# Layer 0 of a two-layer transformer kernel: attention and its following blocks traced in the order of a clock kept in the kernel

## The chip, the cores and the metric

The kernel runs on one core of a Trainium2 chip. A core has five engines that run side by side, each working through its own queue strictly in order: TensorE (PE, matrix products and transposes; weight loads are shown apart as PEld), VectorE (DVE), ScalarE (ACT), GpSimd (POOL) and SyncE (SP, which here only issues DMAs). ACT and POOL issue some DMAs too. Engines wait for each other through semaphores. The metric is the device time of one execution in microseconds (us).

## The reference, cut to what matters

The input x has 4 sequences of 512 positions and 512 features. Four blocks follow each other; every one is `x = x + layernorm(f(layernorm(x)))`, and layernorm has no gain or bias:

```python
x = x + _layernorm(_L0_attn_ref(_layernorm(x), Wq, Wkv, Wo))        # 32 heads of 16, one shared k and v, ALiBi, causal
x = x + _layernorm(_L0_ffn_ref(_layernorm(x), q_scales, q_vals, bias))  # one dequantised 512x512 product plus a bias
x = x + _layernorm(_L1_attn_ref(_layernorm(x), Wq, Wkr, Wdk, Wupk, Wupv, Wo))  # 32 heads of 128, 8 key heads, rope
x = x + _layernorm(_L1_ffn_ref(_layernorm(x), w_gate, w_up, w_down))    # gated, ternary octonion weights
```

Everything is float32. A product in the kernel takes both factors as a rounded high part and a low part and sums three matmuls (high by high, high by low, low by high).

## The kernel before, in words

The program is unrolled in Python and then ordered per engine by a scheduler in the compiler, which follows the order of tracing as a priority and simulates the engines. So the order in which Python emits instructions matters, but an engine's queue may differ from it.

There are three phases. Phase A (classes `A1` and `A2`) does all of layer 0, and also the weight products and the value projection of layer 1's attention. Phase B (`phase_b`) does layer 1's attention and phase C (`C`) its feed-forward block. In the profile phase B's first matmul stands at 727.8 us, and phase A's last matmuls lie just behind it.

**Attention in phase A.** A batch (sequence) has four groups of eight heads, m = 0 to 3. `front` normalises and transposes a batch's x and makes keys and values, `qproj` makes the queries of one group and stores them in DRAM, and `qload` loads them back, rearranged, into the buffer `QS[m]`. The scores are computed twice. `max_tile` (L422, L426) makes them with queries on the partitions, and DVE reduces each tile to a row maximum (L430). `max_end` transposes 32 columns of maxima (L439) and writes them by an ACT-issued DMA into a row of `QS`, so that a second product gives scores with the maximum already taken off. `exp_tile` makes that product with keys on the partitions (L467), ACT takes the exponential (L470), and POOL masks the diagonal tile (L472). `pv` multiplies by values (L483), and `o_piece` transposes the result back (L500) and divides by the sum. There are 128 steps u (a head for the maxima, a block of keys for half a group for the exponentials).

**Posts.** `A2.post(b, t)` takes 128 rows through everything that follows: product with Wo, `add_norm`, feed-forward product with bias (L818), `add_norm`, storing x2 and the transposed normalised x, and two value products for layer 1. `add_norm` is a chain: DVE statistics, aggregate and an add (`ln_gen`, L102 to L106), a power on POOL (L108), a tiny DVE operation (L111), ACT scales and shifts (L727), POOL adds the residual (L729), a second `ln_gen`, and ACT again (L733). `A2.weights` makes combined weights for layer 1 (`products`) and splits the weights of the posts (`setup`); posts wait for it.

**What sets the order.** All of this work is Python generators. `A1.run` walks u from 0 to 140 with the exponentials a fixed 12 steps behind the maxima (`LAG`), four sub-steps each; in each sub-step it emits one maximum tile, gives every waiting generator one turn (`slot`), emits one exponential tile, and gives another turn. A generator spaces itself by counting turns: `hop(n)` lets n turns pass. The exponential tiles have a raised priority (`prio`). Two post streams share the first three batches' twelve posts, and the four posts of the last batch run as four generators with banks and buffers of their own (`room`).

**Banks.** PSUM has eight banks: three for maxima (`ps`), two for exponentials (`pt`), one for probability-by-value sums (`po`), two (`mm`) for everything else. After step 130 three in five exponential tiles take a `ps` bank. `Tok` counts free banks and buffers.

Of the kernel before, what the change touches and what calls it, by code (L numbers as in the profile page):

```python
# [20 lines left out]
B, S, D = 4, 512, 512  # L21
NT = B * S // 128
# [64 lines left out]
class Hop:  # L87

    fine = True

    def __call__(self, n, coarse=0):
        for _ in range(n if self.fine else coarse):
            yield


hop = Hop()


def ln_gen(nc, c, pool, src):

    st = pool.tile([128, 6], F32, name="ln_st", tag="ln_st")
# [7 lines left out]
    yield from hop(3)  # L109
    nm = pool.tile([128, 1], F32, name="ln_nm", tag="ln_nm")  # L110
    nc.vector.scalar_tensor_tensor(nm, mv[:, 0:1], -1.0, rs, ALU.mult, ALU.mult)  # L111
    return rs, nm


class Tok:


    def __init__(self, n):
        self.n = n

    def take(self):
        while self.n == 0:
            yield
        self.n -= 1

    def give(self):
        self.n += 1


class Bank:  # L130
# [9 lines left out]
    def give(self):  # L140
        self.tok.give()


def transpose_gen(nc, c, bank, src, dst_h, dst_l):
    ps = yield from bank.take([128, KC, 128])
    for k in range(KC):
        nc.tensor.transpose(ps[:, k, :], src[:, bass.ts(k, 128)], c.ident)
    yield from hop(1)
    nc.scalar.copy(dst_h, ps)
    yield from hop(2)  # L150
    nc.vector.tensor_tensor(dst_l, ps, f(dst_h), ALU.subtract)
    bank.give()
    yield from hop(1, 1)


def mm3_gen(nc, ps, lh, ll, rh, rl, ks, hops=2, stop=True):
    n = len(ks)
    for j, k in enumerate(ks):
        nc.tensor.matmul(ps, lh(k), rh(k), start=(j == 0), stop=False)  # L159
        nc.tensor.matmul(ps, lh(k), rl(k), start=False, stop=False)  # L160
        nc.tensor.matmul(ps, ll(k), rh(k), start=False, stop=(stop and j == n - 1))  # L161
        yield from hop(hops)
# [24 lines left out]
class Gens:  # L187


    def __init__(self):  # L190
        self.q = []

    def add(self, *gs):
        self.q += gs

    def step(self, n=1):
        for _ in range(n):
            if not self.q:
                return
            g = self.q.pop(0)  # L200
            try:
                next(g)
                self.q.append(g)
            except StopIteration:
                pass

    def drain(self):
        while self.q:
            self.step()


# [4 lines left out]
class A1:  # L216


    def __init__(self, tc, nc, c, aps, o_d, xtp, wqp, P):
# [14 lines left out]
        self.mmp = c.mmp  # L234
# [4 lines left out]
        self.projected = self.exped = self.maxed = self.fronted = self.turn = self.ended = 0  # L239
# [60 lines left out]
    def front(self, b, x):  # L300
# [3 lines left out]
        if x is None:  # L304
# [3 lines left out]
            yield from hop(8)  # L308
        while self.projected < 4 * b:
            yield  # L310
# [3 lines left out]
        for t in range(4):  # L314
# [8 lines left out]
            yield from hop(2)  # L323
# [6 lines left out]
        else:  # L330
# [3 lines left out]
                           lambda k: xt_h[:, k], lambda k: xt_l[:, k], range(KC))  # L334
        vt = self.qp.tile([32, S], F32, name="vt", tag="ql")
        nc.scalar.copy(vt, ps[32:64])
        yield
        for two in range(2):
# [3 lines left out]
            yield from hop(3)  # L342
# [3 lines left out]
            yield  # L346
        if spare:
            psv = self.psT.tile([128, 4, 32], F32, name="ptv", tag="pt")
        else:
            tok.give()  # L350
            yield from tok.take()
            psv = mmp.tile([128, 4, 32], F32, name="mmv", tag="mm")
        for t in range(4):
            nc.tensor.transpose(psv[:, t], vt[:, bass.ts(t, 128)], c.ident[:32, :32])
        vx = self.vp.tile([128, 4, 32], F32, name="vx", tag="vx")
        nc.gpsimd.memset(vx, 1.0)
        yield
        nc.vector.tensor_copy(vx[:, :, 0:16], psv[:, :, 16:32])
        if not spare:
            tok.give()  # L360
        self.vx[b] = vx

    def qproj(self, b, m):
        nc = self.nc
        while self.fronted <= b:
            yield
# [6 lines left out]
        self.projected += 1  # L373
        qh = self.qp.tile([128, S], F32R, name="qh", tag="qh")
        nc.scalar.copy(qh, ps)
        yield from hop(2)
        ql = self.qp.tile([128, S], F32R, name="ql", tag="ql")
        nc.vector.tensor_tensor(ql, ps, f(qh), ALU.subtract)
        self.tok.give()
        dh = self.dp.tile([128, S], F32, name="qh_d", tag="qh_d")  # L380
        nc.sync.dma_start(dh, f(qh))
        dl = self.dp.tile([128, S], F32, name="ql_d", tag="ql_d")
        nc.sync.dma_start(dl, f(ql))
        self.q_d[b, m] = dh, dl

    def qload(self, b, m):
        nc = self.nc
        while (b, m) not in self.q_d:
            yield
        dh, dl = self.q_d.pop((b, m))  # L390
        while self.exped < 32 * (b - 1) + 8 * m + 8:
            yield
# [16 lines left out]
    def max_tile(self, b, m, j, q):  # L409

        nc = self.nc
        two, pr = j // 4, j % 4
        ks = self.KS[b]
        if j == 0 and q == 0:
            assert (b, m) in self.queries
            self.mn = self.sm.tile([128, 8, 4], F32, name="mn", tag="mn", bufs=2)
# [10 lines left out]
        for jj, qb, p in todo + [(j, qb, p)]:  # L427
            nk = 128 * (qb + 1)
            jk = self.jp.tile([128, 512], BF, name="jk", tag="jk")
            nc.vector.tensor_tensor_reduce(  # L430
                out=jk[:, :nk], in0=p, in1=self.c.mask[:, 384 - 128 * qb:512],
                scale=-1.0, scalar=3e38, op0=ALU.add, op1=ALU.min,
                accum_out=self.mn[:, jj, qb:qb + 1])

    def max_end(self, m, mn):
        nc = self.nc
        yield from self.tok.take()
        pm = self.mmp.tile([32, 128], F32, name="mm", tag="mm")
        nc.tensor.transpose(pm, mn.rearrange("p a b -> p (a b)"), self.c.ident)  # L439
        yield  # L440
        mt = self.sm.tile([32, 128], F32R, name="mt", tag="mt", bufs=2)
        nc.scalar.copy(mt, pm)
        self.tok.give()
        for two in range(2):
            r = 64 * two + 58
            nc.scalar.dma_start(f(self.QS[m][r:r + 1]), f(mt[16 * two:16 * two + 16]))
        self.maxed += 8

    def exp_tile(self, v, q):
# [945 lines left out]
```

## Time and profile before

| | us |
|---|---|
| median of 3 runs | 2410.93 (2410.16 to 2412.91) |
| profiled execution | 2413.31 |
| its span, first to last instruction | 2411.6 |
| PE busy in the span | 2301.8 (95%) |
| DVE busy | 1573.0 (65%) |
| POOL busy | 1190.3 (49%) |
| ACT busy | 1076.9 (45%) |
| first score matmul of layer 0 (L422) | at 40.2 |
| first post's first transpose (L147 on po_ot) | at 263.9 |
| last maximum tile (L426) | at 582.4 |
| last exponential tile (L467) | at 667.1 |
| first key projection of layer 1 (L182 on wk_h) | at 727.8 |

The profile is of one execution. A line of a group names the kernel's line, the engine, the operation, output and inputs with shapes, the count, then busy us, mean ns of one, and the idle time of that engine just before, with what ended it. PE's matmuls are pipelined and their ends are modelled, so PE's busy time is an upper bound of its work. The granted clock (PEclk) is the share of full speed that PE was given.

### The profile page before, as it was taken

What the parts mean: (1) busy time and instruction counts of PE and PEld (TensorE: products, weight loads), DVE (VectorE), ACT (ScalarE), POOL (GpSimd) and SP (SyncE); (2) the same over time, 40 slices, a digit from 0 to 9 for tenths busy, and PEclk for the clock granted to TensorE, in tenths of its full rate; (3) what the DMA queues carried; (4) which work ended last, traced back from release to release, by engine and by line L of the source; (5) the groups of instructions that cost most, each with busy time, mean ns of one, the idle gap of its engine ahead of it and who ended that gap; (6) DMA issues with size and microseconds to landing.
All of it is one profiled execution on the core that took longest, in us unless ns stands there. A gap on an engine that the chain in (4) does not pass through costs nothing.

```text
span 2411.6 us, 35873 instructions
## 1 busy us (share of the span) xinstructions
PE 2301.8 (95%) x11606; PEld 1794.2 (74%) x11606; DVE 1573.0 (65%) x4631; ACT 1076.9 (45%) x2404; POOL 1190.3 (49%) x1387
## 2 busy tenths in 40 slices
PE   6899889988889999999999999999999999999998
PEld 4566455555557788888888888888888888878886
DVE  7766656555356777777777767777777778764443
ACT  3555445545543344444444444444444445453332
POOL 3323333434343676566566566666656667522221
PEclk8899899999999999999999999999999999999999
DMA  8845434343367432233122222232222222041000
GB/s 183 238 145 181 98 92 111 89 106 110 94 188 207 135 103 75 88 101 102 66 88 105 70 88 97 79 106 70 88 97 79 91 85 79 14 127 57 31 27 18
DMA packets 158558, 241.54 MB, mean 100 GB/s; under 512 B 26738, under 2 KB 91506, under 8 KB 149540
## 3 DMA queue, kind: packets, MB, share of 16 engines
q1 hardware_dynamic: 141748, 202.42, 27.9%
q0 software_dynamic: 14768, 35.92, 5.3%
q8 instruction: 93, 1.52, 0.3%
q10 hardware_dynamic: 1856, 0.92, 0.2%
q14 instruction: 93, 0.76, 0.1%
HBM read 183.17 MB, written 63.92 MB: 102 GB/s over the span
## 4 chain that ended last, share of the span: by engine, by line
PE 84%; issue 4%; DMA 4%; DVE 3%; POOL 2%; ACT 2%; SPq 1%; ACTq 0%; POOLq 0%; DVEq 0%
PE mm L182 11%; PE mm L184 11%; PE mm L183 11%; PE pt L989 6%; PE mm L159 3%; PE pt L467 3%; PE po L483 3%; PE po L1002 3%; PE po L1003 3%; PE mm L161 3%; PE po L1004 3%; PE mm L160 3%; PE ps L969 3%; PE ps L970 3%; PE ps L971 3%
## 5 line engine op out<-in xcount | busy, mean ns | idle before, releaser
L980 POOL TENSOR_TENSOR s<-s,r 128x384 f32<-128x384 f32 (+3 forms) x512 | 359.6, 722 | 130.0 <-DVE r L979 119.7
L977 ACT ACTIVATE s<-s,mn 128x384 f32<-128x384 f32 (+3 forms) x512 | 286.0, 560 | 223.8 <-DVE mn L973 215.9
L863 POOL TENSOR_TENSOR rp_a<-rp_a,rp_b 128x512 f32<-128x512 f32 x155 | 200.3, 1292 | 262.3 <-DVE rp_b L862 247.5
L992 ACT CAST ph<-pt 128x512 fp32r<-128x512 f32 x320 | 181.7, 586 | 295.5 <-PE pt L989 287.8
L430 DVE CUSTOM_DVE_ANT_0 jk<-ps,mask 128x384 bf16<-128x384 f32 (+3 forms) x512 | 227.5, 483 | 81.2 <-PE ps L426 72.1
L993 DVE TENSOR_TENSOR pl<-pt,ph 128x512 fp32r<-128x512 f32 x320 | 216.5, 686 | 43.4 <-ACT ph L992 40.4
L973 DVE CUSTOM_DVE_ANT_0 s<-ps,mask 128x384 f32<-128x384 f32 (+2 forms) x384 | 203.1, 552 | 37.7 <-PE ps L971 19.5
L470 ACT ACTIVATE pe<-pt 128x512 f32<-128x512 f32 x307 | 174.4, 600 | 97.0 <-PE pt L467 92.7
L989 PE MATMUL pt<-ident,s 128*128 128x128 f32 x1280 | 214.1, 272 | 0.7 <-POOL s L980 0.5
L182 PE MATMUL mm<-xh,w_h 128*128 128x512 f32 x512 | 205.4, 401 | 2.1 <-DVE rp_b L862 1.9
L182 PE MATMUL mm<-w_h,oh 128*128 128x512 f32 x512 | 203.7, 398 | 0.7 <-ACT oh L1008 0.7
L184 PE MATMUL mm<-xh,w_l 128*128 128x512 f32 x512 | 203.6, 398 | 0.0
L183 PE MATMUL mm<-xl,w_h 128*128 128x512 f32 x512 | 202.1, 395 | 0.0
L183 PE MATMUL mm<-w_l,oh 128*128 128x512 f32 x512 | 201.7, 394 | 0.0
L184 PE MATMUL mm<-w_h,ol 128*128 128x512 f32 x512 | 200.3, 391 | 0.0
L989 PEld LDWEIGHTS pt<-ident,s 128*128 128x128 f32 x1280 | 164.7, 140 | 46.1 <-POOL s L980 1.1
L865 POOL TENSOR_TENSOR ql<-rp_a,qh 128x512 fp32r<-128x512 f32 x124 | 160.5, 1294 | 49.6 <-ACT qh L864 49.6
L472 POOL TENSOR_SCALAR_AFFINE_SELECT pe<-pe 128x512 f32<-128x512 f32 x128 | 82.5, 647 | 195.7 <-ACT pe L470 195.1
L859 DVE TENSOR_TENSOR rp_a<-mm,cosq 128x512 f32<-128x512 f32 x128 | 88.4, 691 | 119.6 <-PE mm L184 94.3
L426 PE MATMUL ps<-KS,QS 128*128 128x256 f32 (+2 forms) x384 | 132.7, 384 | 19.2 <-DVE mn L430 18.7
L108 POOL TENSOR_TENSOR ln_rs<-ln_ve,mhalf 128x1 f32<-128x1 f32 x112 | 63.8, 575 | 173.0 <-DVE ln_ve L106 145.5
L1008 ACT CAST oh<-po 128x512 fp32r<-128x512 f32 x128 | 74.5, 582 | 166.1 <-PE po L1004 165.9
(359 smaller groups left out, 5872.5 us busy)
## 6 DMA issues: line engine op xcount, KB each, us to landing
xh<-xt SPq DMA_DIRECT2D x32, 1024.0 KB
xl<-xt SPq DMA_DIRECT2D x32, 1024.0 KB
vh<-v SPq DMA_DIRECT2D x32, 256.0 KB
vl<-v SPq DMA_DIRECT2D x32, 256.0 KB
raw<-in_a_wo SPq DMA_DIRECT2D x32, 256.0 KB
w_h<-in_a_wo POOLq DMA_DIRECT2D x32, 256.0 KB, 3.2
m_d<-t_d SPq DMA_DIRECT2D x192, 42.5 KB
QS<-qh_d SPq DMA_DIRECT2D x62, 128.0 KB
```

Source lines behind the costliest of these rows:

```text
L182: nc.tensor.matmul(ps, lh(k), rh(k), start=(j == 0), stop=False)
L183: nc.tensor.matmul(ps, lh(k), rl(k), start=False, stop=False)
L184: nc.tensor.matmul(ps, ll(k), rh(k), start=False, stop=(j == n - 1))
L430: nc.vector.tensor_tensor_reduce(out=jk[:, :nk], in0=p, in1=self.c.mask[:, 384 - 128 * qb:512], scale=-1.0, scalar=3e38, op0=ALU.add, op1= ...
L470: nc.scalar.activation(e, ps, AF.Exp)
L863: eng.tensor_tensor(a, a, r, ALU.add)
L973: nc.vector.tensor_tensor_reduce(out=s[:, :nk], in0=ps[:, :nk], in1=mask, scale=-1.0, scalar=3e38, op0=ALU.add, op1=ALU.min, accum_out=mn)
L977: nc.scalar.activation(s[:, :nk], s[:, :nk], AF.Exp, bias=mn, scale=-1.0, accum_out=l)
L980: nc.gpsimd.tensor_tensor(s[:, :nk], s[:, :nk], r.to_broadcast([128, nk]), ALU.mult)
L989: nc.tensor.transpose(pt[:, j], PS[u, qb, j][:, bass.ts(kb, 128)], c.ident)
L992: nc.scalar.copy(ph, pt)
L993: nc.vector.tensor_tensor(pl, pt, f(ph), ALU.subtract)
```

## The change

The change replaces the hand-counted order of phase A by a list order made while tracing.

- `Clock` holds a time for each engine and, for each tile, when it was last written and last read. `lengths` gives a duration for each instruction from its engine and its free size, `book` advances the engine and the tiles. `TimedCore` wraps the engines so that every instruction in phase A's `run` is booked, and also chained by `issue_after` behind the previous one on its engine: the compiler's scheduler can no longer change the order within phase A. `TimedPool` gives a reused buffer the time at which its oldest use ends.
- `Streams.run` holds ranked generators. At each turn it takes the generator of best (lowest) rank whose inputs are ready by the clock at PE's time; if none is, it moves to the soonest. `wait(n, tiles)` yields the time the tiles are ready; without a clock (before `run`, and in phases B and C) it lets n turns pass as `hop` did.
- Ranks: query and value weight loads 0; reductions and exponentials on DVE and ACT 1; row maxima and probability-by-value 2; projections, weights, head outputs and posts 3; the maxima's matmuls 4, or 6 when they are `LEAD` = 14 steps ahead of the exponentials; the exponentials' matmuls 4. `LAG`, `slot`, `prio` and the borrowed `ps` banks go.
- Four post streams, one for each row block t, go through all four batches in the same code. They share three pairs of transposed tiles and, for the first three batches, the two `mm` banks; the last batch's streams have a bank each.
- `add_norm` no longer forms the shifted sum: one DVE operation makes `y * rs + x`, which differs from it by a constant per row, and the next normalisation removes that constant. The two shifts are added back once, when x2 is stored, by one extra ACT pass and one tiny DVE add per post.

```diff
+LEAD = 14
+class Clock:
+    def ready(self, *aps):
+        return max((self.done.get(a.tensor.name, 0.0) for a in aps), default=0.0)
+    def lengths(self, e, op, out, ins, kw):
+        n = out.free_size()
+        if op == "dma_start":
+            issue = {self.SP: 0.4, self.ACT: 0.55, self.POOL: 0.7}[e]
+            return issue, issue + 2.2 + 4e-5 * out.size() / 4
+        if e == self.PE:
+            n = 0.108 if op == "transpose" else 0.018 + 0.417e-3 * n
+            return n, n + 0.2
+        if e == self.ACT:
+            n = 0.2 + 0.78e-3 * n + 0.2 * (len(ins) > 2)
+            return n - 0.12, n + 0.03
+        if e == self.DVE:
+            n = 0.15 + 1.05e-3 * max(n, max((a.free_size() for a in ins), default=0))
+            return n - 0.08, n + 0.03
+        n = 0.56 if n == 1 else 0.05 + (1.15e-3 if op != "tensor_tensor" else 2.4e-3) * n
+        return n - 0.05, n + 0.08
...
+class Timed:
...
+            with ck.tc.issue_after(ck.last[e]) if e in ck.last else nullcontext():
+                r = fn(*a, **k)
+            ck.last[e] = r.ins
+            ck.book(e, op, outs, pos + ins, k)
...
+class Streams:
+    def run(self):
+        ck = self.ck
+        while self.q:
+            now, best, soonest = ck.now(), None, float("inf")
+            for s in sorted(self.q, key=lambda s: (s[0](), s[1])):
+                t = s[3]() if s[3] else 0.0
+                if t < soonest:
+                    best, soonest = s, t
+                if t <= now:
+                    break
+            ck.t = max(now, soonest)
+            try:
+                best[3] = next(best[2])
+            except StopIteration:
+                self.q.remove(best)
...
-    def run(self, extra):
-        LAG = 12
-        total = 32 * B
-        self.gens += [self.projections(), self.loads()]
-        for u in range(total + LAG + 1):
...
+    def run(self, ck, starts):
+        self.nc = TimedCore(ck, self.nc)
+        self.streams = Streams(ck)
+        self.rank = self.streams.add
+        self.begun = lambda u: [self.rank(*g) for g in starts.get(u, [])]
+        for m in range(4):
+            ck.done[self.QS[m].tensor.name] = 3.0 * m
+        self.rank(0, self.loads())
+        self.rank(2, self.outputs())
+        self.rank(3, self.projections())
+        self.rank(lambda: 4 if self.heads < self.exped + LEAD else 6, self.maxima())
+        self.rank(4, self.exponentials())
...
-    def add_norm(self, y, x, bank, o, new_xn):
+    def add_norm(self, y, x, bank, o):
         nc, c = self.nc, self.c
-        rs, nm = yield from ln_gen(nc, c, self.sm, y)
-        o = o()
-        nc.scalar.activation(o, y, AF.Identity, bias=nm, scale=rs)
-        bank.give()
-        nc.gpsimd.tensor_tensor(o, o, x, ALU.add)
-        rs, nm = yield from ln_gen(nc, c, self.sm, o)
-        xn = new_xn()
-        nc.scalar.activation(xn, o, AF.Identity, bias=nm, scale=rs)
+        rs, mv = yield from rstd_gen(nc, c, self.sm, y)
+        yield from wait(1, rs, x)
+        nc.vector.scalar_tensor_tensor(o, y, rs, x, ALU.mult, ALU.add)
+        bank.give(y)
+        shift = ln_shift(nc, self.sm, rs, mv)
+        rs, mv = yield from rstd_gen(nc, c, self.sm, o)
+        yield from wait(1, rs)
+        return shift, rs, ln_shift(nc, self.sm, rs, mv)
...
     def post(self, b, t):
...
-        x2, xn = yield from self.add_norm(y, x1, bank, r.x2, r.n2)
-        out = nc.sync if last else nc.gpsimd
-        out.dma_start(self.x2_d[bass.ts(T, 128), :], x2)
-        xh, xl = yield from r.pair("x2")
-        yield from transpose_gen(nc, c, bank, xn, xh, xl)
+        s2, rs, nm = yield from self.add_norm(y, y1, bank, x)
+        yield from wait(0, nm)
+        nc.scalar.activation(y1, x, AF.Identity, bias=nm, scale=rs)
+        shift = self.sm.tile([128, 1], F32, name="shift", tag="shift")
+        nc.vector.tensor_tensor(shift, s1, s2, ALU.add)
+        xh, xl = yield from self.pair()
+        yield from transpose_gen(nc, c, bank, y1, xh, xl)
+        nc.scalar.activation(x, x, AF.Identity, bias=shift)
...
     def posts(self):
-        todo = [(b, t) for b in range(B - 1) for t in range(4)]
-        def stream():
-            while todo:
-                yield from self.post(*todo.pop(0))
-        return [stream(), stream()] + [self.post(B - 1, t) for t in range(4)]
+        def stream(t):
+            for b in range(B):
+                yield from self.post(b, t)
+        return [(3, stream(t)) for t in range(4)]
...
-            start = {4: [a2.weights()], 5: [a2.load_wv()], 6: a2.posts()}
-            a1.run(lambda u: start.get(u, []))
+            a2 = A2(tc, TimedCore(ck, nc), c, aps, a1, o_d, x2_d, xt_d, v_d, wk_d, wv_d, P1)
+            a1.run(ck, {4: [(3, a2.weights())], 5: [(0, a2.load_wv())], 6: a2.posts()})
```

## The prediction

> **What bounds the kernel now.** First the page's row of slices: after slice 13 (about 780 us) TensorE (PE) is 90% busy or more in every slice, and those two thirds are not in the diff. Before, it falls to 8, and its granted clock with it.
>
> ```profile
> PE   6899889988889999999999999999999999999998
> PEclk8899899999999999999999999999999999999999
> ```
>
> So I cut layer 0 into windows (columns: stretch, length, busy us and instructions of PE, PEld, DVE, ACT, POOL, then PE clock, DMA share, GB/s).
>
> ```profile
> 100.00:720.00 620.00, 560.57 (x3028) 357.46 (x3028) 355.04 (x1355) 309.30 (x559) 220.79 (x305) 0.96 0.45 124
> 140.00:220.00 80.00, 79.86 (x450) 56.11 (x449) 45.93 (x173) 38.58 (x72) 15.13 (x20) 1.00 0.43 133
> 240.00:280.00 40.00, 32.06 (x162) 16.65 (x159) 25.04 (x109) 16.39 (x30) 12.26 (x16) 0.83 0.51 122
> 580.00:720.00 140.00, 117.36 (x577) 76.07 (x577) 55.76 (x154) 64.11 (x109) 58.56 (x79) 0.94 0.46 139
> ```
>
> PE leaves 59 us idle in 100-720, but busy overstates: an isolated matmul is drawn 0.40 long, while in an unbroken run the next starts after 0.23. I therefore count work by spacing at full clock, from PE's timeline of 100-720: 1360 matmuls 512 wide at 0.233 (starts 590.87 to 592.27, six of them) make 317; 77 of 384 at 0.178, 14; 205 of 256 at 0.12, 25; 339 transposes at 0.09, 30; the probability-by-value groups at 0.99, 0.78, 0.57 and 0.35 per eight, 86. That is **472 us of work in 620 us: 0.76**. The same count gives 0.94 for 140-220 (projections, weight products and attention all ready), 0.79 for 300-580, 0.54 for 240-280 (attention alone) and 0.69 for 580-720. DVE is at 57%, ACT 50%, POOL 36%: no engine but PE is near its limit, so the lost 148 us are order and latency.
>
> Who holds PE, from the waits of 100-670 (us in total, times, longest):
>
> ```profile
> PEld ps L426 <- DVE mn L430: 31.1, 53, 6.5
> PEld pt L467 <- ACT pe L470: 22.1, 46, 1.1
> PEld mm L147 <- ACT xn L733: 16.6, 8, 4.5
> ```
>
> These are the maxima's and exponentials' banks, and transposes behind a norm: each a matmul queued before its input while other work was ready. Two places in the timeline show what that costs. First, a load holds DVE at the head of its queue, and all engines stop for 6.5 us:
>
> ```profile
> 247.51 1.06 PE L483 MATMUL po<-pe,vx 128*32 128x512 f32 x8
> ...
> 252.93 0.69 DVE L718 SCALAR_TENSOR_TENSOR x<-x,xn 128x512 f32<-128x512 int32 x1 [7.06 <-DMA xn<-in_f_s]
> ...
> 254.15 1.41 PE L426 MATMUL ps<-KS,QS 128*128 128x384 f32 x2 [5.58 <-DVE mn L430]
> ```
>
> Second, two short gaps halve the clock (starts 0.43 apart):
>
> ```profile
> 643.96 0.66 PE L147 MATMUL mm<-ident,xn 128*128 128x128 f32 x4 [1.70 <-ACT xn L733]
> 645.56 0.80 PE L159 MATMUL mm<-wv_h,x2h 128*128 128x512 f32 x1 [0.95 <-ACT x2h L149]
> 646.16 0.63 PE L160 MATMUL mm<-wv_l,x2h 128*128 128x512 f32 x1
> 646.59 0.63 PE L161 MATMUL mm<-wv_h,x2l 128*128 128x512 f32 x1
> ```
>
> Over 100-720 the clock shortfall in 20 us windows sums to 28 us.
>
> **The change part by part.** The sum is made against the profiled execution: 2413.3 us, span 2411.6 and 1.7 around it; the median of the runs is 2410.9, 2.4 less.
>
> *Order (the main term).* No matmul is added or removed. The kernel's clock traces an instruction when its inputs are done by its own account, and chains each engine to that order. Its durations fit the rows: exponential 0.60 booked, 0.60 measured; 512-wide DVE subtract 0.69 and 0.69; POOL add 1.28 and 1.28; pow 0.56 and 0.57; matmul 0.23 and 0.23; SP issue 0.4 and 0.42. The last 50 us of work are the final batch's four posts, four alike chains in both orders; 680-720 ran at 0.70, I take 0.75 for a shorter chain: 50/0.75 = 67. The other 422 us lie between 0.79, where posts and attention mix today (no gain), and 0.94, where enough is ready. I take the middle, 0.865, because the clock removes waits for DVE and ACT but not the chains: 488. Together 555 against 620: **65 us less**.
>
> *Normalisation.* By group rows of 100-730:
>
> ```profile
> L733 ACT ACTIVATE xn<-x,ln_nm,ln_rs 128x512 f32<-128x512 f32 x24 | 19.5, 813 | 24.6 <-DVE ln_nm L111 22.7 <-issue 1.2 <-DVE mn L430 0.6
> L727 ACT ACTIVATE x<-mm,ln_nm,ln_rs 128x512 f32<-128x512 f32 x24 | 18.6, 776 | 10.8 <-DVE ln_nm L111 10.5
> ```
>
> From y to xn today: statistics 0.69, aggregate 0.18, add 0.15, pow 0.57, shift 0.22, ACT 0.78, POOL add 1.28, the first five again 1.81, ACT 0.81: 6.5 us. Afterwards one DVE operation (0.69 by the PSUM subtract, 0.91 by the integer form; I take 0.69, same types) replaces ACT and POOL add: 5.1. 32 norms take 41 us off POOL and 25 off ACT, add 16 x 0.78 = 12 to ACT and 22 to DVE plus 16 tiny adds (2). DVE then has 379 us in 555, 68%: hidden. The 2 x 1.4 us a post show only in the tail and are in my 0.75.
>
> *Four streams, three pairs, two shared banks.* A post holds a bank about 27 us (three transposes at 2.0: 0.4 PE, 0.6 ACT, 0.7 DVE and hand-overs; two products at 6.3: 2.8 and the first half of a norm; two value products at 4.3), 326 us for twelve posts; with projections, weights and head outputs about 550, over two banks 275 of 555: no bound, 0 us. If that cover went, a bank at 70% would cost what 580-640 shows.
>
> *Queues.* Per early post POOL still issues five DMAs (0.56-0.77 each), SP four value stores (0.36); the x2 store now follows the xt stores and one more ACT pass, read only hundreds of us later. A late result holds what is behind it on SP, the QS loads among them; they can go once the previous batch's eight steps on that buffer are exponentiated, with about 10 of the 128 score steps (over 40 us) in hand, against 3.4-6.8 us for those QS loads whose landing the trace shows. Zero, bounded by the 12.5 us that exponentials waited for QS today, either way. The final exponentials lose the three spare score banks: two banks need 0.52 us an exponential, ACT 0.60, so ACT hides it.
>
> *Start, 40-100.* DVE stood 9.3 us on an x load and PE 8.3 on DVE. The clock books that landing at 3.3 us and can neither foresee it nor avoid it: 0 taken, 8 either way.
>
> *Phases after 780:* same code, no term.
>
> [...] The granted clock dropped after gaps of 1.44, 1.70 and 0.95 us within 6 us. [...]
> POOL's 256 KB loads of x landed in 2.9-5.9 us. [...]
>
> **Rivals.**
> *Full recovery.* 422 us at 0.94 and the tail at 0.80: 449 + 62 = 511, 109 less: 2304 (2298-2318). For it: DVE and ACT have room. Against: the norm chains stay.
> *Attention left alone.* Posts rank above attention: a batch's posts (50 us of PE) finish early, and the next batch's attention (58 us) fills only a quarter of that time, 16 us; the other 42 us, in three batches, run alone. 240-280 without its 6.5 us stop ran at 0.64: 126 x (1/0.64 - 1/0.865) = 51 given back: 2399 (2375-2408). For it: DVE needs four reductions of 0.48 + 0.08 = 2.2 us a step (128 steps), PE 1.83 (233 us of scores and values over 128). Against: the maxima may now run 14 steps ahead.
> *Landings misjudged, slower.* Every engine is chained to the clock's order, so a booked 3.3 us landing that takes 7-12 stops ACT or DVE and soon PE, 6.5 us as at 247.5. Today three waits are that long (11.6, 9.3, 7.1). Some 60 weight, x and post loads could do it; from 11 new stops it is slower, with 12: 2348 + 78 = 2426 (2418-2440).
> *No effect.* The compiler's scheduler already ordered the queues; if it ends alike, 2413.
>
> **How the numbers follow.** Forecast 2413.3 - 65 = 2348, its own range 2318-2375: 0.47. Full recovery 0.15, attention alone 0.18, slower 0.16, no effect 0.04. Range 2298 to 2426 leaves out half of the slower case and little below. About 0.2% (5 us) is what a measurement of this kernel can tell from no change. Faster 0.80, same 0.04, slower 0.16.
>
> **What would show it.** Right: layer 1's first key projection, 727.8 us now, starts 55-75 us earlier; PE in 100-650 at 0.85 by spacing; waits of L426 on DVE under 15 us; clock 0.98 or more; POOL adds of L729 gone, DVE near 68%. Attention alone: windows with score work only and PE below 0.7. Slower: waits over 5 us of ACT or DVE for loads of weights or x, PE idle behind them. I am wrong if phases after the projection start also move, or if PE's waits only change names.

## The result, and the profile after

The kernel after takes 2430.75 us (median of 4 runs, 2426.32 to 2435.66) against 2410.55 us before (also 4 runs): a ratio of 1.0082, 95% interval 1.0068 to 1.0096. It is 20 us slower, where 65 us less had been forecast. Its profiled execution took 2432.1 us, span 2430.4.

The page's slices (TensorE's busy tenths, then its granted clock), to be held against the same two rows of before:

```profile
PE   6799899998888999999999999999999999999998
PEclk8899899999999999999999999999999999999999
```

The dips have moved, not gone: slices 6 and 9 are up from 8 to 9, slice 2 is down to 7 and slice 13 to 8, and 10 to 12 still stand at 8. The windows of the kernel after, with the columns of the prediction's windows:

```profile
100.00:720.00 620.00, 568.10 (x3015) 357.81 (x3014) 372.65 (x1368) 292.09 (x541) 181.46 (x277) 0.96 0.45 128
140.00:220.00 80.00, 76.06 (x407) 49.14 (x407) 50.54 (x200) 39.51 (x73) 21.11 (x27) 1.00 0.49 127
240.00:280.00 40.00, 32.90 (x153) 18.37 (x153) 31.59 (x128) 21.04 (x38) 23.05 (x28) 0.79 0.61 187
580.00:720.00 140.00, 120.42 (x632) 72.86 (x631) 59.63 (x171) 65.47 (x118) 42.97 (x67) 0.97 0.40 120
```

PE had 3015 matmuls in 100-720 against 3028, at the same mean clock, 0.96. VectorE is up and ScalarE and GpSimd are down, as the short normalisation wants. The best stretch of before, 140-220, was hurt: 407 matmuls in place of 450. PE's waits in 100-670 of the kernel after (us in total, times, longest):

```profile
PEld ps L167 <- DVE mn L167: 31.3, 64, 3.6
PEld pt L167 <- ACT pe L167: 20.8, 44, 2.3
```

Every operation that goes by the clock now carries the helper's line, 167, so one goes by tiles. The first wait was 31.1 us before, the second 22.1: neither has changed. Only the norm groups look as planned. Here are three of them (columns as on the page, 100-730). The first is the pass that stood before as L733 (813 ns), the second is the new late shift, and the third takes the place of ScalarE's pass from PSUM, L727 (776 ns), and of GpSimd's add; the same operations also stand under other buffer letters:

```profile
L167 ACT ACTIVATE A<-B,ln_nm,ln_rs 128x512 f32<-128x512 f32 x16 | 13.0, 815 | 27.7 <-DVE ln_nm L167 27.7
L167 ACT ACTIVATE A<-A,shift 128x512 f32<-128x512 f32 x14 | 10.3, 736 | 0.0
L167 DVE SCALAR_TENSOR_TENSOR A<-mm,ln_rs,B 128x512 f32<-128x512 f32 x13 | 9.7, 747 | 3.2 <-POOL ln_rs L167 3.2
```

To see where the 20 us came from I use one measure for all kernels: PE's work, counted by spacing at full clock as in the prediction, summed from the start, and for each amount the time at which each kernel has reached it. The lag is that time less the time of before. Read at before's 60, 100, 260, 580, 720, 800 and 2350 us (each from one profiled execution, so a few us of scatter):

| kernel | 60 | 100 | 260 | 580 | 720 | 800 | 2350 |
|---|---|---|---|---|---|---|---|
| after | +21 | +10 | +27 | +13 | +8 | +17 | +19 |
| e_pe_chain | +18 | +11 | +28 | +15 | +8 | +17 | +22 |
| e_late_chain | +17 | +7 | +10 | -2 | -9 | -2 | -2 |
| e_early_chain | +21 | +9 | +21 | +12 | -7 | +4 | +4 |
| e_free | +15 | +3 | +4 | -3 | -22 | -17 | -9 |
| e_x2 | +21 | +11 | +27 | +8 | +1 | +10 | +14 |
| e_free_x2 | +15 | +3 | +3 | -17 | -26 | -20 | -15 |
| e_free_x2_two | +16 | +4 | +3 | -31 | -36 | -24 | -19 |

The kernel after is 27 us late by 260 us, makes up 24 by 540 (+3 there), and loses again at 540-580 and at the seam between the layers, 760-780. After that little changes.

Two places are plain in the timeline of the kernel after (start, duration, engine, operation, and in brackets the idle time and what ended it). ScalarE stands 20.5 us for the first weight load, which SP issued only at 59.83, behind loads of the queries and of x and other copies:

```profile
55.92 0.84 SPq L564 DMA_DIRECT2D QS<-ql_d  x2
56.80 1.94 SPq L1281 DMA_DIRECT2D t_d<-tpm  x3
58.84 0.94 SPq L167 DMA_DIRECT2D x<-in_x  x1
59.83 2.19 SPq L167 DMA_DIRECT2D raw<-in_a_wdk  x4
68.13 2.47 ACT L167 CAST wd_h<-raw 128x512 fp32r<-128x512 f32 x4 [20.49 <-DMA raw<-in_a_wdk]
...
763.75 0.56 SPq L167 DMA_DIRECT2D xt<-ph  x1
765.29 0.55 SPq L167 DMA_DIRECT2D xt<-pl  x1
767.95 0.33 SPq L167 DMA_DIRECT2D x_d<-A  x1
768.33 4.99 SPq L1291 DMA_DIRECT2D m_d<-t_d  x8
770.64 0.59 ACT L167 CAST A<-po 128x512 fp32r<-128x512 f32 x1 [5.71 <-DMA x_d<-A]
```

The last lines are the seam: the last post's value copy writes the tile A that the x2 store (x_d<-A) still reads, and that store is now behind the xt stores, those of the transposed normalised x.

### The profile page after: what moved, and what is told of

It reads as the page before. It is cut to its first block, busy times and chain, and to the rows that moved or that the text cites. A ratio compares the mean times of both kernels' runs of the same rounds, so it can differ in the third digit from the quotient of the medians.

```text
span 2430.4 us, 35931 instructions
## 1 busy us (share of the span) xinstructions
PE 2317.4 (95%) x11606; PEld 1795.4 (74%) x11606; DVE 1593.5 (66%) x4679; ACT 1064.7 (44%) x2388; POOL 1147.1 (47%) x1355
## 4 chain that ended last, share of the span: by engine, by line
PE 80%; DMA 5%; issue 5%; DVE 5%; ACT 2%; SPq 2%; POOL 1%; ACTq 0%; POOLq 0%; DVEq 0%
PE mm L354 11%; PE mm L355 10%; PE mm L356 10%; PE mm L167 10%; PE pt L1142 5%; PE pt L167 3%; PE po L167 3%; PE po L1155 3%; PE po L1156 3%; PE po L1157 3%; PE ps L1122 3%; PE ps L1123 3%; PE ps L1124 3%; PE gu L1361 3%; PE gu L1362 3%
## 5 line engine op out<-in xcount | busy, mean ns | idle before, releaser
L167 DVE CUSTOM_DVE_ANT_0 jk<-ps,mask 128x384 bf16<-128x384 f32 (+3 forms) x512 | 221.5, 486 | 47.1 <-PE ps L167 41.2
L167 ACT ACTIVATE pe<-pt 128x512 f32<-128x512 f32 x320 | 179.5, 601 | 96.9 <-PE pt L167 86.6
L1142 PE MATMUL pt<-ident,s 128*128 128x128 f32 x1280 | 208.5, 272 | 0.2 <-DVE pl L1146 0.2
L167 PE MATMUL ps<-KS,QS 128*128 128x256 f32 (+2 forms) x448 | 140.1, 394 | 46.4 <-DVE mn L167 35.6
L167 POOL TENSOR_TENSOR ln_rs<-ln_ve,mhalf 128x1 f32<-128x1 f32 x76 | 42.1, 553 | 240.5 <-DVE ln_ve L167 232.9
L167 PEld LDWEIGHTS ps<-KS,QS 128*128 128x128 f32 x448 | 85.9, 209 | 89.1 <-DVE mn L167 54.7
```

The source lines that it names most:

```text
L167: r = fn(*a, **k)
L1142: nc.tensor.transpose(pt[:, j], PS[u, qb, j][:, bass.ts(kb, 128)], c.ident)
```

## The experiments

Sixteen kernels were run. A ratio is to the kernel before; 0.001 is 2.4 us.

**1. The chains to the clock's order.** e_free drops them; the trace order stays, and the compiler's scheduler may reorder within it. (What differs is who makes the order of each engine's queue.)

```diff
-            with ck.tc.issue_after(ck.last[e]) if e in ck.last else nullcontext():
-                r = fn(*a, **k)
+            r = fn(*a, **k)
```

> The kernel after, but no instruction is chained to the one that the clock traced before it on its engine: the trace order stays, the compiler's scheduler may reorder it as it did before the change. Theory 'forced order': the chains turn every late landing into a stop of an engine (ScalarE 20.5 us at 47.6-68.1 us, a post 5.7 us at 770). Freed, the layer comes back to what the kernel before had or better: 2395 to 2415 us, first key projection before 725. Theory 'the order itself': the ranks decide which work is there, the scheduler keeps most of it: 2425 to 2435, full-rate share of PE in 100-580 again near 0.80.

Measured: 2407.9 us, 0.9977 (0.9964 to 0.9990). Against 1.0082 the chains cost 0.0105, 25 us. Windows of e_free:

```profile
100.00:720.00 620.00, 575.27 (x3107) 377.55 (x3106) 379.12 (x1386) 295.07 (x541) 179.31 (x271) 0.98 0.46 131
140.00:220.00 80.00, 77.91 (x432) 53.18 (x431) 51.21 (x196) 41.96 (x78) 18.69 (x26) 0.98 0.43 110
580.00:720.00 140.00, 129.06 (x659) 87.61 (x658) 68.44 (x183) 61.79 (x108) 38.87 (x60) 1.00 0.51 151
```

The forced-order theory had its time right, and its mark, a first key projection before 725, came earlier still (699.3): of the 22 us lead at 720 more than half is gone at the end, 5 us of it by 800 and 8 behind that. Which engine's chain is it? e_pe_chain keeps PE's alone:

```diff
-            with ck.tc.issue_after(ck.last[e]) if e in ck.last else nullcontext():
+            with ck.tc.issue_after(ck.last[e]) if e in ck.last and e == ck.PE else nullcontext():
```

> The kernel after, with the chain of each instruction to the one traced before it kept on PE alone; ScalarE, VectorE, GpSimd and the SP queue are free for the scheduler. Without any chain the time was 0.9977 of before, with all of them 1.0082. Theory 'PE's order': PE is the engine that is short, and its fixed order makes every late input a hole in it: most of the 25 us is still lost, 1.005 to 1.009. Theory 'the other queues': late landings and late banks stop ScalarE, VectorE and SP at the head of their queues, and PE only feels it; with these free PE's fixed order costs little: 0.996 to 1.001.

Measured: 1.0109 (1.0086 to 1.0132), above even the range of its first theory: PE's order alone loses all of it. ScalarE's long stop isn't needed for it: here it waited about half as long for that first weight load and had other work before, and PE was as late at 100 us.

```profile
70.66 2.49 ACT L167 CAST wd_h<-raw 128x512 fp32r<-128x512 f32 x4 [11.06 <-DMA raw<-in_a_wdk]
```

Where in the layer? Chains only from the weights' products on (e_late_chain), or only up to them (e_early_chain):

```diff
+        self.chain = False
...
-            with ck.tc.issue_after(ck.last[e]) if e in ck.last else nullcontext():
+            with ck.tc.issue_after(ck.last[e]) if e in ck.last and ck.chain else nullcontext():
...
         yield from self.products()
+        wait.clock.chain = True
```

> The kernel after, where the chains to the clock's order begin only when the weights' products have been traced (about 230 us). Theory 'start': the loss of the clock's order lies before that (27 us behind the kernel before at 260 us); without chains there the start runs like the kernel without chains, and the clock's order gains afterwards as it did (19 us from 260 to 760): 0.990 to 0.998. Theory 'whole layer': the order loses everywhere and the scheduler wins everywhere: 1.003 to 1.008.

> The reverse: chained to the clock's order until the weights' products have been traced, free from then on. Theory 'start': the 27 us of the first 260 us are lost, and the scheduler makes good no more after that than the clock's order did: 1.004 to 1.010. Theory 'whole layer': 1.000 to 1.004.

Measured: 0.9993 (0.9982 to 1.0004), between the ranges of its two theories, and 1.0046 (1.0030 to 1.0061). Late chains cost 0.0016 over none, 4 us (the intervals overlap); early ones 0.0069, 17 us. So most of the chains' loss is the order of about the first 230 us, as the start theory has it; but its other half, that the clock's order wins afterwards, falls (0.9993 is no better than no chains at all).

**2. Correcting the clock.** If the early loss comes from wrong times, right ones should mend it. e_start gives the clock the start as the trace shows it, e_dma a longer landing:

```diff
-            ck.done[self.QS[m].tensor.name] = 3.0 * m
+            ck.done[self.QS[m].tensor.name] = (0.0, 6.0, 10.0, 23.0)[m]
+        ck.at[ck.SP] = 20.0
```

```diff
-            return issue, issue + 2.2 + 4e-5 * out.size() / 4
+            return issue, issue + 4.0 + 4e-5 * out.size() / 4
```

> The kernel after, but its clock is told what the trace shows of the start: SP is busy for the first 20 us, and the four QS tiles of batch 0 are there at 0, 6, 10 and 23 us instead of 0, 3, 6 and 9. Theory 'start': PE's work is 10 us late at 100 us because the first weight load is queued behind SP's earlier loads and ScalarE, chained to it, stands 20.5 us; with the right times the exponentials go first, that stop is under 5 us, and 6 to 10 us are saved: 2420 to 2425. Theory 'made up later': the lag is only moved, since the weights' work still has to be done before 300 us: 2428 to 2434.

> The kernel after, with every load and store booked 1.8 us longer on its clock (4.0 instead of 2.2 us after the issue), nearer to the 4.2 to 5.8 us in which GpSimd's loads of the posts landed in 100-760. Theory 'landings': PE's order is bad because inputs come later than booked; with the longer booking work that is there is put ahead, the time falls by 8 to 20 us, 1.000 to 1.005. Theory 'one constant is never right': what the loads miss is queueing (20 us at the start, 3 to 9 us elsewhere), not a constant; the order only changes: 1.005 to 1.012.

Measured: e_start 1.0162 (1.0147 to 1.0178), outside both theories; e_dma 1.0066 (1.0053 to 1.0080), not to be told from the kernel after. e_start did mend the start: its lag at 60 is 10 us instead of 21. But from before's 220 to 260, which are its own 236 to 302 us, the lag grew from 16 to 42 us. PE's timeline of e_start there:

```profile
252.64 0.80 PE L167 MATMUL pt<-QS,KS 128*128 128x512 f32 x1 [4.11 <-ACT pe L167]
...
279.78 1.11 PE L167 MATMUL mm<-ident,B 128*128 128x128 f32 x4 [6.35 <-DMA B<-o_d]
...
290.46 1.52 PE L167 MATMUL ps<-KS,QS 128*128 128x256 f32 x4 [9.56 <-DMA wk_l<-wk_d]
```

Three stops, 20 us, two of them put down to transfers: the order that fits the start collides with others. The loads of the posts' x did land later than before, by the DMA answers of 100-760 of before and after (256 KB each, the last figure is the median us from issue to landing):

```profile
xr<-in_x POOLq DMA_DIRECT2D x12, 256.0 KB, 3.1
```

```profile
A<-in_x POOLq DMA_DIRECT2D x12, 256.0 KB, 5.8
```

but booking every load and store 1.8 us longer moved the time by an unresolved 0.0016.

**3. Ranks.** e_exp25 puts the exponentials ahead of the posts.

```diff
-        self.rank(4, self.exponentials())
+        self.rank(2.5, self.exponentials())
```

> The kernel after with the exponentials ranked ahead of the posts and weights (2.5 instead of 4). Theory 'attention alone': posts first leave score work alone at 640-700, PE's matmuls 0.64 apart in rate; with exponentials first the last one comes 20 us or more earlier than 685.5 and layer 0 ends earlier: 2410 to 2422. Theory 'posts' chain': the posts are the longer chain and become late instead (the kernel's own clock ends at 650.9 instead of 633.0): 2440 to 2455, the last bias matmul after 760.

Measured: 1.0209 (1.0194 to 1.0224); the last exponential came later, not earlier, at 715 instead of 685, and the time left even the range of the posts' theory. Against 1.0082 it is 31 us worse. But by the lag all of that is there by before's 300 us (+49 against +18 in the kernel after), when its first posts have just begun: the weights' products, which the new rank also puts behind the exponentials, ended at 283.5 instead of 231.2, and the posts wait for the weights, so that the first post's first transpose came at 325.5 instead of 275.7. From before's 300 to 720 both kernels make up some 10 us. So the 31 us are not the price of exponentials ahead of posts; where posts run, that rank showed no gain and no loss.

**4. The place of the x2 store.** e_x2 is the kernel after with the store ahead again, e_free_x2 the same without chains.

```diff
         nc.scalar.activation(x, x, AF.Identity, bias=shift)
+        yield from wait(0, x)
+        queue.dma_start(self.x2_d[bass.ts(T, 128), :], x)
         for i, e in enumerate((xh, xl)):
             yield from wait(0, e)
             queue.dma_start(self.xt_d[i][b][:, :, bass.ts(t, 128)], f(e))
-        yield from wait(0, x)
-        queue.dma_start(self.x2_d[bass.ts(T, 128), :], x)
```

> The kernel after with the store of x2 (and its ScalarE pass) issued again ahead of the two xt stores. Theory 'reuse': the value product's high half overwrites the tile that this store reads; it waited 5.7 us for it in the last post and 4.3 us in earlier ones, on the path that ends layer 0, so the seam to layer 1 gets 5 to 8 us shorter: 2422 to 2426, no wait of the last posts on a DMA from that tile over 1 us. Theory 'own order': the seam is set by the number of posts still open when the exponentials end, the wait goes to the next thing: 2428 to 2433.

> No chains, and the x2 store again ahead of the xt stores. Theory 'two separate losses': the store's move cost 10 us with the chains (1.0082 to 1.0042) and costs as much without them, since the last posts' value products overwrite the tile it reads in either case: 0.9977 less 0.003 to 0.004, so 0.9935 to 0.9950. Theory 'one loss': without chains something else runs in that wait, the store's place is worth nothing: 0.997 to 0.999.

Measured: 1.0042 (1.0025 to 1.0059) and 0.9942 (0.9922 to 0.9963), 0.0040 and 0.0035 less than with the store behind: 8 to 10 us, and beside the chains, not in place of them. That copy in e_x2's timeline:

```profile
761.25 0.59 ACT L167 CAST A<-po 128x512 fp32r<-128x512 f32 x1 [1.72 <-PE po L167]
```

It now waits for its own product. The table puts the gain of e_x2 earlier than I had thought: it is there by 720 (+1 against +8), and the seam itself, 720 to 800, costs 9 us in both. So the wait at 770 only marks the fault; the gain comes from about 540 us on, while the posts of the third and fourth batches run. ScalarE has two more such waits in the kernel after, and none in e_x2:

```profile
642.94 0.59 ACT L167 CAST A<-mm 128x512 fp32r<-128x512 f32 x1 [1.66 <-DMA x_d<-A]
652.58 0.59 ACT L167 CAST A<-mm 128x512 fp32r<-128x512 f32 x1 [2.67 <-DMA x_d<-A]
```

The three make 10.0 us, but about 5 of the gain are there by before's 580, ahead of the first of them. The place of the store is priced; that these waits are all of its price is not shown, for the clock's order moved with it.

e_free_x2_su takes one more stop out of the seam. VectorE stood 9.64 us in e_free_x2 on a product of two scales that the last phase wants, because, as the wait suggests, its tile lies where a store of the last post's values was still reading; that store was on SP behind copies of the last phase's weights (m_d):

```profile
730.21 8.20 SPq L1290 DMA_DIRECT2D m_d<-t_d  x8
738.52 0.53 SPq L166 DMA_DIRECT2D v<-ph  x1
739.09 1.15 SPq L1290 DMA_DIRECT2D m_d<-t_d  x2
740.34 0.52 SPq L166 DMA_DIRECT2D v<-pl  x1
746.41 0.16 DVE L1337 TENSOR_TENSOR su<-sc 128x1 f32<-128x1 f32 x1 [9.64 <-DMA v<-pl]
```

```diff
-        su = sm.tile([128, 1], F32, name="su", bufs=1)
-        nc.vector.tensor_tensor(su, sc[:, 1:2], sc[:, 2:3], ALU.mult)
+        su = sc[:, 3:4]
...
                 tern.store(c)
+            nc.vector.tensor_tensor(sc[:, 3:4], sc[:, 1:2], sc[:, 2:3], ALU.mult)
```

> No chains, the x2 store ahead of the xt stores, and the product of two scales for the last phase (1 element a partition) is taken right after the scales are known instead of where that phase's pools are opened. In the kernel without this last edit VectorE stood 9.6 us on it at 736.8-746.4, for its tile lies where the last post's store of values had not landed, and PE 7.9 us behind VectorE. Theory 'head of the queue': that stop goes, 6 to 8 us less: 0.9942 to about 0.991. Theory 'seam': the rotations and stores of the seam need that time anyhow, 0 to 2 us less: 0.9935 to 0.9945.

Measured: 0.9937 (0.9922 to 0.9952) against 0.9942: nothing that can be told. That stop went, and GpSimd got one of 8.24 us. The profile puts it down to one of those copies; the load that it needs, raw, was issued only at 759.36, behind thirteen of them:

```profile
747.83 11.43 SPq L1290 DMA_DIRECT2D m_d<-t_d  x13
759.36 0.53 SPq L1053 DMA_DIRECT2D raw<-in_a_wo  x1
762.52 1.26 POOL L1054 TENSOR_TENSOR w_l<-raw,w_h 128x512 fp32r<-128x512 f32 x1 [8.24 <-DMA m_d<-t_d]
```

**5. The short normalisation.** e_oldnorm puts the old one into the kernel after, e_free_oldnorm into the one without chains, e_shortnorm the short one into the kernel before (with a GpSimd copy of each shift beside it, and the turns of `hop` counted anew).

```diff
-        nc.vector.scalar_tensor_tensor(o, y, rs, x, ALU.mult, ALU.add)
-        bank.give(y)
         shift = ln_shift(nc, self.sm, rs, mv)
+        yield from wait(0, shift)
+        nc.scalar.activation(o, y, AF.Identity, bias=shift, scale=rs)
+        bank.give(y)
+        yield from wait(0, o)
+        nc.gpsimd.tensor_tensor(o, o, x, ALU.add)
```

> The kernel after with the normalisation of before (ScalarE and a GpSimd add in place of one VectorE operation, no late shift, x2 complete before its transposes). Theory 'hidden': 1.4 us per norm is beside other work but in the last batch's posts: the time rises by 0 to 6 us, 1.0082 to 1.011. Theory 'chain counts': the posts' chains set the middle too, 32 norms x 1.4 us over four streams, 11 us or more: 1.013 or above. It also brings the x2 store's data 1 pass earlier, but leaves the store behind the xt stores.

> No chains, and the normalisation of before. Theory 'chained order': a longer norm is felt because the posts rank first and PE's order is fixed (16 us with the chains); without chains other work is put in its place, as in the kernel before, where the short norm gained nothing (1.0013): 0.9977 to 1.0005. Theory 'four streams': the posts' chains decide with four alike streams in any order, and the 16 us show again: 1.003 to 1.006.

> The kernel before with the short normalisation alone (one VectorE operation for ScalarE's pass and GpSimd's add; x2 is completed by a ScalarE pass ahead of its store); streams, banks and order as before. In the order of the clock the short chain was worth 16 us (1.0149 against 1.0082). Theory 'chain': a post is 2 x 1.4 us shorter in any order: 0.993 to 0.998. Theory 'hidden': the other order of before hides it and only the last posts gain, 2 to 4 us: 0.998 to 1.000.

Measured: e_oldnorm 1.0149 (1.0124 to 1.0173), e_free_oldnorm 1.0036 (1.0023 to 1.0050), e_shortnorm 1.0013 (1.0004 to 1.0022). The short norm is worth 0.0067 with the chains to the clock's order and 0.0059 without, 14 to 16 us; in the kernel before it gains nothing and costs 3. So it isn't the fixed order that lays the norms open. It seems to go with what these two kernels share and before lacks: the clock's trace order, four alike streams, three pairs, two banks. Which of these was not separated, nor what the copy and the new turns cost in e_shortnorm.

**6. Two post streams.** e_two runs two in the first three batches; e_free_x2_two adds that to e_free_x2.

```diff
-            for b in range(B):
+            for b in range(B - 1):
                 yield from self.post(b, t)
+                yield from self.post(b, t + 2)
 
-        return [(3, stream(t)) for t in range(4)]
+        return [(3, stream(t)) for t in range(2)] + [(3, self.post(B - 1, t)) for t in range(4)]
```

> The kernel after with two post streams for the first three batches (tiles 0 and 2, 1 and 3 one behind the other) and four for the last one, as before the change. Theory 'four alike streams cost': four posts of a batch stand in the same chains at once, ahead of the exponentials, and leave score work alone at 640-700; with two they spread into the next batch's attention: 8 to 15 us less, 1.002 to 1.005. Theory 'streams don't matter': what is lost lies in the first 260 us (24 of the 17 us net), where no post runs: 1.006 to 1.010.

> No chains, the x2 store ahead, and two post streams for the first three batches. Theory 'streams cost': the 6 us of two streams under the chains (1.0055 against 1.0082) come on top: 0.991 to 0.993. Theory 'no cost': the scheduler spreads the posts itself: 0.994 to 0.996.

Measured: 1.0055 (1.0040 to 1.0070) and 0.9913 (0.9896 to 0.9929), 0.0027 and 0.0029 less than their kernels with four. Each pair of intervals touches, but both say 7 us; 1.0055 lies between the ranges of e_two's theories. Where it comes from shows at 540-560. There PE has attention alone in the kernel after (the first line); in e_two (the second) 24 value products and 4 transposes of posts stand between:

```profile
540.00:560.00 20.00, 16.32 (x92) 7.52 (x90) 11.15 (x48) 9.77 (x19) 8.89 (x16) 0.93 0.63 160
540.00:560.00 20.00, 18.32 (x114) 11.50 (x109) 11.63 (x49) 10.79 (x22) 8.18 (x14) 1.00 0.82 234
```

By spacing that is 0.60 against 0.81, and from before's 540 to 580 the lag grows by 10 us in the kernel after and by 2 in e_two. e_free_x2_two, 2393.4 us, beats both kernels: by the ratios 21 us under before and 41 under after. Its windows:

```profile
100.00:720.00 620.00, 582.41 (x3177) 393.29 (x3176) 389.05 (x1408) 299.79 (x550) 180.52 (x273) 0.98 0.48 137
240.00:280.00 40.00, 37.30 (x198) 25.47 (x198) 26.29 (x105) 19.30 (x35) 12.56 (x20) 0.91 0.48 133
```

It issues 149 matmuls more in 100-720 than before and starts the first key projection at 685.6, 42 us earlier; of its lead of 36 us at 720 the seam takes 12 back by 800, and 5 more are gone by 2350.

**7. What holds the middle.** e_shortmax takes each maximum over 128 keys only and leaves out the rest of the reduction.

```diff
-                nk = 128 * (qb + 1)
+                nk = 128
...
-                    out=jk[:, :nk], in0=p, in1=self.c.mask[:, 384 - 128 * qb:512],
+                    out=jk[:, :nk], in0=p[:, 128 * qb:], in1=self.c.mask[:, 384:512],
```

> The kernel after, where each maximum is taken over the last 128 keys of its block alone instead of up to 512 (part of the computation is left out): VectorE's reductions get shorter, PE's work stays. PE's waits on the maxima's banks were 31 us in 100-670 before and after. Theory 'maxima': VectorE's share of a score step (2.2 us against PE's 1.8) holds the attention, so the middle stays at 0.80 whatever the order; with short reductions the waits of PE on them fall below 15 us and the time by 25 to 40 us: 0.992 to 0.998. Theory 'chains': PE waits for exponentials, transposes and posts in turn, these take the place; the kernel's own clock ends 14 us earlier, and no more than 5 to 14 us are saved: 1.002 to 1.006.

Measured: 1.0046 (1.0028 to 1.0065), 9 us less, and 6 of them are there by 100 us. PE's waits, 100-670:

```profile
PEld ps L167 <- DVE mn L167: 6.2, 19, 0.8
PEld pt L167 <- ACT pe L167: 29.8, 55, 2.4
```

VectorE lost 70 us of work (302 against 373 in 100-720) and PE's wait on the maxima 25 us, and 9 us came of it: the wait on the exponentials grew by 9, for one. A total of PE's waits under one name is not a price.

## Why the prediction was wrong

**What bounds the kernel: right.** The 472 us of full-rate PE work in 620 is 477 in the kernel after: 0.77, as 0.76 before. Two readings of mine were a little off and change nothing: the last slice of the page is at 8, and taken one by one there are 114 and 170 matmuls of 384 and 256 columns, not 77 and 205, which makes the 472 about 475.

**The order term failed.** This is the step that turned 65 us less into 20 more: it let the layer run at 0.865, the middle of 0.79 and 0.94, because the clock would remove the waits for VectorE and ScalarE, and it gave nothing below today's rates. Measured by the same spacing: 140-220 fell from 0.94 to 0.83, 300-580 went from 0.79 to 0.80 and 580-720 from 0.69 to 0.71. The waits stayed (31.3 and 20.8 us against 31.1 and 22.1). The marks I had set failed with it: the first key projection starts at 729.0 (727.8 before), PE's wait on the maxima is 31 us and not under 15, the clock 0.96 and not 0.98. I took the good rate of 140-220 as a ceiling to rise to; it was a thing to lose. The kernel's clock replaced the scheduler's order there, and PE's new order cost 25 us, some 17 to 21 of them early. Where posts and attention mix, the lag did fall by 24 us from 260 to 540, but with the old norm (e_oldnorm) by 10 only, so more than half of that is the norm and not the order. Even the best order run here, e_free_x2_two, reached 0.83 over 100-720. An estimate, if the pieces add: of its 21 us, 14 are the short norm's worth without chains, and 7 are left for the clock's trace order, where 65 were forecast. That the durations booked fit the rows said nothing of when inputs are there.

**The norm at nothing but the tail: mis-sized.** The one VectorE operation took 0.75 us, against my 0.69; but the shorter chain is worth 14 to 16 us here. Nor is that the tail: with the chains, e_oldnorm is 3 us behind the kernel after at before's 300 us and 14 behind at 400, among the first batch's posts. The cover that I named, other work, does not hide it in these kernels; in the kernel before the short norm gained nothing.

**Four streams at 0: mis-sized,** by 7 us. My bank count asked only whether the banks suffice, not what four alike chains do to the order: a batch's posts end together and attention is left alone, as at 540-560.

**The x2 store moved at 0: failed.** I asked who reads x2 ("hundreds of us later") and not who next writes the tile it is read from: the same post, two steps later. Its place is worth 8 to 10 us.

**The start at 0, 8 either way:** 10 us late at 100. Without chains it is 3, with PE's chain alone 11, so some 7 are PE's order. That the order is late because the clock knows nothing of SP's queue is not shown: told of it, e_start was 11 us better at 60, but 3 at 100. **Phases after 780, no term:** they lose 2 us; the seam, in no term, loses 9 at 720-800.

**The rivals.** The slower rival's number, 2418 to 2440, holds the time, but by luck. Its root was that a fixed order cannot answer to late inputs. That a fixed order costs is shown; that late inputs are why is not. Its mechanism fails: it wanted 12 stops of 6.5 us on ScalarE or VectorE, and from 40 to 800 us the kernel after has two over 5 us for such loads (20.5 ending at 68 and 8.8 at 130); PE's chain alone loses as much with those engines free, and the waits for loads that stop PE itself stay small (the largest in 100-720 is 3.4 us in all, on the queries). "Attention left alone" holds in part: its sign, score work alone with PE below 0.7, stands in the kernel after at 540-560 (0.60) and 660-680 (0.62). Two streams mend the first of these, and the price is nearer their 7 us than its 51. "Full recovery" was reached by no order that was run.

**What stays open:** why PE's order by the clock is slow before 230 us, and which inputs, if any, are late there. Of two corrections of the clock one changed nothing that can be told and the other made it worse.

## What to carry to other kernels

Price an imposed order from both sides: the stretch that runs at 0.94 under the old order is the first that a new one can lose, and durations that fit the rows do not yet make a model's order better than that of the scheduler it replaces. When a store is moved back, look for who next overwrites its source, not only for who reads its result. A wait total or a single stop names a place; only an experiment gives its price: here a stop of 9.6 us went and brought nothing that can be told, and 25 us of waits went and brought 9.

## What was not expected of the hardware

In the records of both kernels the granted clock is either full or half. In 100-720 of the kernel after seven spells at half begin, 3.4 to 10.2 us long and 47.8 us in all, so 24 us are lost; in the kernel before it is twelve, in the same range of lengths and 54.6 us in all. The longest gap in the records of PE and its weight loads in that stretch of the kernel after is 3.3 us. Gaps of 1.2 us at 639.7 and 1.1 us at 473.1 were each followed by such a spell within 2 us (the mean granted clock was 0.74 in 644-648 and 0.67 in 474-478), while gaps of 1.4 us at 412.6 and 1.6 us at 529.2 were not (1.00 in 413-417 and in 530-534). So the length of a gap alone does not tell in these records whether a half follows, and the prediction's "two short gaps halve the clock" is what one place of the kernel before showed, no more. What decides it was not shown; no run was made to test it. One such spell in the timeline of the kernel after (starts 0.43 apart, where those from 637.18 to 637.88 are 0.23 apart at full clock):

```profile
640.85 0.50 PE L167 MATMUL pt<-QS,KS 128*128 128x512 f32 x1 [1.16 <-ACT pe L167]
...
643.24 0.63 PE L167 MATMUL mm<-wv_l,ph 128*128 128x512 f32 x1
643.67 0.63 PE L167 MATMUL mm<-wv_h,pl 128*128 128x512 f32 x1
```
